# Loading batch 0 in four pieces, the taps ahead of conv1's weights, and one step of the taps' transform in front of the first transposes

## The chip, the cores and the metric

The kernel runs on one core of a Trainium2 chip. The metric is the device time of one execution in microseconds (us). The kernel before takes 1845.73 us, median of its first three runs (1843.53 to 1846.13). All runs told of here are of the state fast. With them comes, to three digits, the mean clock granted to TensorE during the run.

## The reference, cut to what matters

One layer of a graph network on 32 graphs of 512 nodes and 256 features, in float32.

```python
h = jnp.maximum(_layernorm(x, axis=-1), 0.0)
# inside the layer, with x now being h:
xc = jnp.transpose(x, (0, 2, 1))
h = relu(_bn(_conv1d(xc, conv1_w, 0), ...))      # a 256 x 256 product per node
h = _bn(_conv1d(h, conv2_w, 8), ...)             # 17 taps along the nodes
x_conv = transpose(relu(h + xc))
# ... message passing over adj, then a GRU cell; the result is added to x
```

## The kernel before

The 17-tap convolution is done by Fourier transforms of windows. Two things have to be transformed: the activations, batch by batch (`px`), and the taps of conv2, once (`pw`). The taps' transform comes in 32 steps of four matmuls each (eight records in the trace), which the kernel spreads over the loop that prepares the first 16 batches. The loop's TensorE work per batch is conv1 (`pc`), a step of the taps, the window transform of the batch before (`px`), a second step, and the transposes of the next batch (`phT`).

One step, and who takes its results out of PSUM (`s` is 0 for an even step and 2 for an odd one):

```python
def weights_to_freq(gen, pc, i):
    s = i % SI                                   # SI = 4 channels to a group of four buffers
    if s == 0:
        for q in range(4):                       # a new group: 8 buffers, so two groups
            WST[q] = gen.tile([ROWS, SI, D], FP, tag="wst", ..., bufs=8)
    for q in range(4):
        p = bank(...)                            # one of 8 PSUM banks
        nc.tensor.matmul(p[:ROWS, :], taps[...], W2P[pc][...], start=True, stop=True)
    for q in range(4):
        if (pc or i >= SI) and (q == 3 or (q == 1 and s == 0)):
            nc.vector.tensor_copy(dst, src)      # even step: two, odd step: one
        else:
            nc.scalar.copy(dst, src)             # even step: two, odd step: three
    if s + per == SI:                            # after the odd step: store the group
        for q in range(4):
            nc.sync.dma_start(WD[...], WST[q]...)
```

The loads at the start, and which steps a batch gets:

```python
nc.scalar.dma_start(vec, vecs)
nc.scalar.dma_start(fwd, ...)                    # window transform
nc.scalar.dma_start(taps, ...)                   # taps' transform
# ... (cut)
load_w1()                                        # conv1's weights, four transfers on ScalarE's queue
load_x(0)                                        # 512 KB each, on SyncE's queue
load_x(1)
load_taps(gen, 0, nc.sync)                       # first 8 of 64 channels per quarter, five transfers

def between(b):
    # ... every second batch: load the next taps; batches 1 to 7: load a late weight
    mine = spread(steps, b, GB - 1) if b < GB - 1 else []
    return mine[:1], mine[1:]                    # one after conv1, the rest after px
```

Of the kernel before, what the change touches and what calls it, by code (L numbers as in the profile page):

```python
# [11 lines left out]
FP = mybir.dt.float32  # L12
# [3 lines left out]
P = 128  # L16
# [49 lines left out]
def gnn_layer(  # L66
# [15 lines left out]
    nc = tc.nc  # L82
    B, N, D = x.shape
# [45 lines left out]
    nc.scalar.dma_start(vec, vecs)  # L129
    w1 = early.tile([P, DC, D], FP, name="w1")  # L130
    fwd = early.tile([P, 2 * L], FP, name="fwd")
    nc.scalar.dma_start(fwd, nc.inline_tensor(fwd_np, name="dft_fwd").ap())
    taps = early.tile([P, ROWS], FP, name="taps")
    nc.scalar.dma_start(taps, nc.inline_tensor(taps_np, name="dft_taps").ap())
    back = consts.tile([P, back_np.shape[1]], FP, name="back")
# [53 lines left out]
    def load_w1():  # L189

        t = W2P["w1"] = pools["gen"].tile([P, PI, D], FP, tag="w2p", name="w1_in", bufs=2)
        load_rows(t[:, :DC], w1T, nc.scalar)

    def scale_w1():
        t = W2P.pop("w1")
# [615 lines left out]
    def first_part(g, freq, between, left=()):  # L811


        b0, b1 = g * GB, (g + 1) * GB
        for b in range(b0, b0 + 3):
            if b not in X and (g == 0 or b == b0):
                load_x(b)
        if g == 0:
            t = XN[b0] = pools["first"].tile([P, NC, D], FP, tag="xn", name="rows", bufs=2)
            ones, diags = t[:, 0, :P], t[:, 1:3, :].rearrange("p i (c m) -> p i c m", m=P)  # L820
            nc.vector.memset(ones, 1.0)

            for _ in range(6):
                nc.tensor.matmul(row1[1][:, : 2 * P], ident, fr.rearrange("p c g k -> p (c g k)")[:, : 2 * P], start=True, stop=True)
            batch_norm("bn1", scale1, shift1, nc.gpsimd)
            bn1_row(0, scale1, ones, diags)
            bn1_row(1, shift1, ones, diags)
        if b0 not in STATS:
            statistics(b0)
        normalise(b0)  # L830
        if g == 0:
            scale_w1()
            shift_w1()
        left = list(left)

        def fill():
            for step in left.pop(0) if left else ():
                step()

        if g > 0:  # L840
            load_x(b0 + 1)
            fill()
            load_x(b0 + 2)
        transpose_h(b0)
        fill()
        statistics(b0 + 1)
        if g > 0:
            statistics(b0 + 2)
        normalise(b0 + 1, g > 0)
        fill()  # L850
        for b in range(b0, b1):
            if b + 3 < b1:
                load_x(b + 3, nc.gpsimd)
            if b == b0:
                conv1(b)
                one, two = between(0) if g == 0 else ([], [])
                for step in one:
                    step()
                fill()
                if g == 0:  # L860
                    transpose_h(b + 1)
                    statistics(b + 2)
                    normalise(b + 2)
                else:
                    normalise(b + 2)
                    transpose_h(b + 1)
                fill()
                xf, last_two = freq(g), two
                continue
            if g == 0 and b == b0 + 1:  # L870
                conv1(b)
                for step in last_two:
                    step()
            if b + 2 < b1:
                statistics(b + 2)
            if b + 1 < b1:
                transpose_h(b + 1)
            if b + 2 < b1:
                normalise(b + 2)
            one, two = between(b - b0)  # L880
            if b > b0 + (g == 0):
                conv1(b)
            if b == b1 - 1:
                load_h(b0)
            for step in one:
                step()
            windows_to_freq(b - 1, xf)
            for step in two:
                step()
        by_chunks(b1 - 1)  # L890
        load_h(b0 + 1)
        windows_to_freq(b1 - 1, xf)
        by_chunks(b0)
        return xf
# [8 lines left out]
    with tc.tile_pool(name="freq", bufs=1) as fpool:  # L903
        def freq_tile(g):
            return fpool.tile([P, DC, L, P], FP, tag="xf", name=f"xf_{g}")

        with phase("first", "gen"):
            gen = pools["gen"]
            per = N // D
            steps = [partial(weights_to_freq, gen, pc, i) for pc in range(QI // PI) for i in range(0, PI, per)]  # L910
            load_w1()
            load_x(0)
            load_x(1)
            load_taps(gen, 0, nc.sync)

            def between(b):
                if b % 2 == 0 and b // 2 + 1 < QI // PI:
                    load_taps(gen, b // 2 + 1)
                if 1 <= b <= len(load_weights):
                    load_weights[b - 1]()  # L920
                mine = spread(steps, b, GB - 1) if b < GB - 1 else []
                return mine[:1], mine[1:]

            with tc.manual_schedule():
                xf = first_part(0, freq_tile, between)

                for u in range(3):
                    load_unit(0, u)


        LEFT = 4

        def nodes(g, xf, units, last):


            b1 = (g + 1) * GB
            todo = [b1 - 1] + list(range(g * GB, b1 - 1))
            def begin(i):
                if i < GB:
                    if todo[i] not in HQ:  # L940
                        by_chunks(todo[i])
                    message(todo[i])
                    features(todo[i])

            load_adj(todo[0])
            with tc.manual_schedule():
                begin(0)
                message(todo[1])
                factors(todo[0])
                features(todo[1])  # L950
            affinity(todo[0])
            for i, b in enumerate(todo):
                mine = spread(units, i, last) if i < last else []
                more = i + 1 < GB

                if g + 1 < NG and i == GB // 2:
                    load_x(b1)
                if g + 1 < NG and i == 3 * GB // 4:
                    statistics(b1)
                if i + 2 < GB and todo[i + 2] not in HT:  # L960
                    load_h(todo[i + 2])
                if more:
                    load_adj(todo[i + 1])
                    factors(todo[i + 1])

                parts = [range(DC)] if mine or not more else [[0], [1]]
                if len(parts) > 1:
                    aggregate(b, parts.pop(0))
                for u in mine[:1]:
                    product(pools["pw"], g, u, xf)  # L970
                begin(i + 2)
                if more:
                    affinity(todo[i + 1])
                for u in mine[1:2]:
                    product(pools["pw"], g, u, xf)
                aggregate(b, *parts)
                save_nmp(b)
                for u in mine[2:]:
                    product(pools["pw"], g, u, xf)

        with phase("pw", "ahead"):
            with phase("nodes"):
                nodes(0, xf, range(UNITS - LEFT), GB)
            with phase("first", "sums"):
                combine = combine_weights()

                def between(b):

                    if b == GB - 3:
                        for u in range(3):  # L990
                            load_unit(1, u)
                    two = [partial(sum_unit, pools["pw"], 1, b - GB + 3)] if b > GB - 3 else []
                    return combine[b - 1] if 0 < b <= len(combine) else [], two


                pw, (u0, u1, u2, u3) = pools["pw"], range(UNITS - LEFT, UNITS)
                left = [[partial(load_unit, 0, u2, pools["sums"])],
                        [partial(prepare, pw, 0, u1, xf), partial(product, pw, 0, u0, xf), partial(prepare, pw, 0, u2, xf)],
                        [partial(product, pw, 0, u1, xf), partial(load_unit, 0, u3)],
                        [partial(prepare, pw, 0, u3, xf), partial(product, pw, 0, u2, xf)],  # L1000
                        [partial(product, pw, 0, u3, xf)]]
                prepare(pw, 0, u0, xf)
                load_unit(0, u1)
                with tc.manual_schedule():
                    xf = first_part(1, freq_tile, between, left)
            with phase("nodes"):
                nodes(1, xf, range(UNITS), GB - 3)
# [76 lines left out]
```

## Time and profile before

| | before |
|---|---|
| median time | 1845.73 us |
| TensorE busy | 99% of the span |
| TensorE in the chain that ended last | 89% |
| batches 2 to 6, each | 9.27 us |
| batch 7 (three steps) | 10.38 us |
| batches 8 to 13, each | 9.66 us |

The time of a batch is the distance between the starts of conv1 of two batches in TensorE's row of the timeline. The lines behind this table are in the prediction below.

### The profile page before, as it was taken

To read this page: it belongs to the slowest core of one execution; us is meant where nothing else is said; L and a number is where in the kernel's file an instruction comes from. 1 tells how busy PE (TensorE), PEld (TensorE's weight loads), DVE (VectorE), ACT (ScalarE), POOL (GpSimd) and SP (SyncE) were. 2 spreads that over 40 slices of the span, in tenths; PEclk is the share of its full clock that TensorE was granted. 3 is DMA by queue.
4 is the path that set the end of the run, shared out by engine and by line. 5 is a ranking of instruction groups with operands and counts; after the bars stand their busy time and mean duration, and the time that the engine had idled before them with its cause. 6 is when DMAs were issued, how large, how long until landed. Compare 5 with 4: busy or idle time off the path is not lost.

```text
span 1848.1 us, 20105 instructions
## 1 busy us (share of the span) xinstructions
PE 1826.4 (99%) x6610; PEld 1089.0 (59%) x6610; DVE 1109.1 (60%) x2220; ACT 581.9 (31%) x1083; POOL 588.2 (32%) x572
## 2 busy tenths in 40 slices
PE   9999999999999999999999999999999999999998
PEld 6777666666888666665555554555455544555443
DVE  7775656554885555545266466655666466645666
ACT  4555434432335333333222221222122221222121
POOL 3331333333432344444422323133212322133221
PEclk9999999999999999999999999999999999999999
DMA  8999888875678887778421443234422442244312
GB/s 233 299 276 241 225 226 246 218 179 180 212 250 207 235 245 235 216 207 261 123 86 34 120 120 99 53 88 120 120 78 43 120 120 88 49 103 120 112 25 52
DMA packets 307452, 289.26 MB, mean 157 GB/s; under 512 B 148028, under 2 KB 237148, under 8 KB 306964
## 3 DMA queue, kind: packets, MB, share of 16 engines
q1 hardware_dynamic: 281300, 224.22, 46.0%
q10 hardware_dynamic: 19024, 38.68, 5.9%
q0 software_dynamic: 7024, 25.07, 4.8%
q8 instruction: 53, 0.87, 0.2%
q14 instruction: 51, 0.42, 0.1%
HBM read 191.50 MB, written 96.40 MB: 156 GB/s over the span
## 4 chain that ended last, share of the span: by engine, by line
PE 89%; DVE 4%; issue 3%; DMA 2%; POOL 1%; ACT 1%; SPq 0%; POOLq 0%; ACTq 0%; DVEq 0%
PE pg L597 29%; PE pn L597 14%; PE pn L489 11%; PE py L393 11%; PE pm L439 6%; PE pc L585 5%; PE pc L328 3%; PE px L343 3%; PE pw L256 2%; PE pd L474 2%; PE phT L312 1%; DMA w<-in_w_ihT_dram 1%; PE psr L463 1%; DVE stats L285 1%; DVE xn L304 1%
## 5 line engine op out<-in xcount | busy, mean ns | idle before, releaser
L489 PE MATMUL pn<-A,msg 128*128 128x512 f32 x512 | 225.9, 593 | 0.6 <-DVE A L480 0.6
L597 PE MATMUL pg<-hp,sw 128*128 128x512 f32 x434 | 221.8, 593 | 0.7 <-DVE rz L616 0.5
L597 PE MATMUL pg<-np,sw 128*128 128x512 f32 x434 | 221.6, 592 | 0.0
L597 PE MATMUL pg<-cp,sw 128*128 128x512 f32 x434 | 221.6, 592 | 0.0
L575 POOL TENSOR_TENSOR hp<-hp 128x512 f32<-128x512 f32 x64 | 81.3, 1280 | 413.0 <-DMA hp<-hd 234.6
L372 POOL TENSOR_TENSOR both<-xf 128x256 f32<-128x256 f32 x78 | 60.1, 771 | 329.1 <-PE py L393 297.5
L489 PEld LDWEIGHTS pn<-A,msg 128*128 128x128 f32 x512 | 97.2, 191 | 110.9 <-issue 105.7
L575 POOL TENSOR_TENSOR cp<-cp 128x512 f32<-128x512 f32 x64 | 80.4, 1267 | 229.8 <-ACT cp L591 228.6
L393 PE MATMUL py<-wt,both 128*128 128x256 f32 x624 | 151.0, 385 | 0.7 <-issue 0.7
L612 ACT ACTIVATE rz<-rz,brz 128x512 f32<-128x512 f32 x93 | 67.0, 721 | 260.2 <-DVE rz L616 260.2
L400 DVE TENSOR_TENSOR y<-y,py 128x256 f32<-128x256 f32 x78 | 31.8, 408 | 190.5 <-ACT y L399 185.8
L597 PEld LDWEIGHTS pg<-hp,sw 128*128 128x128 f32 x434 | 82.2, 190 | 104.8 <-issue 97.8
L597 PEld LDWEIGHTS pg<-cp,sw 128*128 128x128 f32 x434 | 82.5, 190 | 103.8 <-issue 103.8
L597 PEld LDWEIGHTS pg<-np,sw 128*128 128x128 f32 x434 | 82.5, 190 | 103.8 <-issue 103.8
L393 PEld LDWEIGHTS py<-wt,both 128*128 128x128 f32 x624 | 114.3, 190 | 43.2 <-issue 28.3
L480 DVE TENSOR_TENSOR A<-e,at 128x512 f32<-128x512 f32 x128 | 114.5, 933 | 36.9 <-ACT e L477 36.7
L359 POOL TENSOR_TENSOR wsum<-wt 128x512 f32<-128x512 f32 x78 | 109.1, 1399 | 51.8 <-DMA wt<-wd 39.1
L735 ACT ACTIVATE nt<-nt,vech 128x512 f32<-128x512 f32 x64 | 46.2, 722 | 235.8 <-DVE nt L734 235.8
L328 PE MATMUL pc<-w,hT 128*128 128x256 f32 x512 | 116.7, 381 | 1.6 <-DVE hT L316 1.6
L439 PE MATMUL pm<-wmsg,hq 128*128 128x259 f32 x512 | 117.5, 382 | 0.6 <-ACT sl L460 0.6
L597 PE MATMUL pn<-np,sw 128*128 128x512 f32 x224 | 114.4, 592 | 0.0
L597 PE MATMUL pn<-cp,sw 128*128 128x512 f32 x224 | 114.4, 592 | 0.0
(146 smaller groups left out, 2963.6 us busy)
## 6 DMA issues: line engine op xcount, KB each, us to landing
wt<-wd SPq DMA_DIRECT2D x160, 256.0 KB, 4.3
adj<-in_adj_dram SPq DMA_DIRECT2D x128, 256.0 KB, 5.4
wd<-wst SPq DMA_DIRECT2D x64, 320.0 KB, 5.3
yd<-y ACTq DMA_DIRECT2D x80, 256.0 KB, 4.3
yt<-yd SPq DMA_DIRECT2D x30, 640.0 KB, 7.5
hd<-hT SPq DMA_DIRECT2D x32, 512.0 KB, 4.4
nd<-nmp ACTq DMA_DIRECT2D x32, 512.0 KB, 4.0
xb<-in_x_dram SPq DMA_DIRECT2D x128, 128.0 KB, 3.8
```

Of the source, the lines that this page charges most:

```text
L328: nc.tensor.matmul(p[:, j, :], HT[b][:, ic, c * P : (c + 1) * P], w1[:, ic, :], start=(ic == 0), stop=(ic == DC - 1))
L343: nc.tensor.matmul(p[:, j * 2 * L : (j + 1) * 2 * L], H1[b][:, c0 + j, ic * P : (ic + 1) * P], fwd, start=True, stop=True)
L359: nc.gpsimd.tensor_tensor(t, WT[g, u][:, 0], WT[g, u][:, 1], op=ALU.add)
L372: nc.gpsimd.tensor_tensor(both[:, 0], re, im, op=ALU.add)
L393: nc.tensor.matmul(dst, v[:, ic, :], w[:, ic, :], start=(ic == 0), stop=(ic == DC - 1))
L439: nc.tensor.matmul(p[:, : D + NS], hq[:, ic, c * P : (c + 1) * P], wmsg[:, ic, :], start=(ic == 0), stop=(ic == DC - 1))
L480: nc.vector.tensor_mul(A[b][:, mc, :], e, at)
L489: nc.tensor.matmul(p, MSG[b][:, mc, dc * P : (dc + 1) * P], A[b][:, mc, :], start=(mc == 0), stop=(mc == NC - 1))
L575: nc.gpsimd.tensor_tensor(t[:, dst, :], t[:, a, :], t[:, b, :], op=sub)
L585: nc.tensor.matmul(bk[:, t0:t1], YT[p][j][:, c, oc * P : (oc + 1) * P], back[:, n : n + t1 - t0], start=(c == 0), stop=(c == len(spans) - ...
L597: nc.tensor.matmul(bk[:, t], sw[:, k, q, o, :], terms[k][q][:, t], start=(first and i == 0), stop=(i == len(ks) - 1), skip_group_check=True)
L612: nc.scalar.activation(rz[:, g, j, :], src, AF.Sigmoid, bias=brz[:, g : g + 1], scale=1.0)
```

## The change

The intent: TensorE stands idle several times in the first 11 us. Batch 0 should come sooner by being split over two queues, its statistics should start with the first piece, and an idle place in front of the first transposes should be filled with a step of the taps that the loop then need not do.

```diff
-    nc.scalar.dma_start(fwd, ...)               # now last on ScalarE's queue
     nc.scalar.dma_start(taps, ...)
 # ... in load_w1
-        load_rows(t[:, :DC], w1T, nc.scalar)
+        load_rows(t[:, :DC], w1T, nc.sync)
 # ... in first_part, group 0
             batch_norm("bn1", scale1, shift1, nc.gpsimd)
+            statistics(b0)
             bn1_row(0, scale1, ones, diags)
             bn1_row(1, shift1, ones, diags)
+            left.pop(0)[0]()                    # step 0 of the taps
 # ... the loads
+            X[0] = pools["first"].tile([P, NC, D], FP, tag="x", name="x_0", bufs=3)
+            for c in range(NC):
+                (nc.sync if c % 2 == 0 else nc.scalar).dma_start(X[0][:, c, :], x[0, c * P : (c + 1) * P, :])
+            load_taps(gen, 0, nc.sync)
             load_w1()
-            load_x(0)
             load_x(1)
-            load_taps(gen, 0, nc.sync)
+            nc.scalar.dma_start(fwd, ...)
 # ... (cut)
-                xf = first_part(0, freq_tile, between)
+                xf = first_part(0, freq_tile, between, [[steps.pop(0)]])
```

A side effect is not visible in the diff: `between` now spreads 31 steps instead of 32. Every batch from 0 to 6 gets the pair (odd, even) where it had (even, odd).

More of the change, by code (lines that the diff above doesn't have):

```diff
@@ L131, in gnn_layer @@
     fwd = early.tile([P, 2 * L], FP, name="fwd")
-    nc.scalar.dma_start(fwd, nc.inline_tensor(fwd_np, name="dft_fwd").ap())
     taps = early.tile([P, ROWS], FP, name="taps")
@@ L817, in first_part @@
                 load_x(b)
+        left = list(left)
         if g == 0:
@@ L833, in first_part @@
             shift_w1()
-        left = list(left)
         def fill():
@@ L910, in gnn_layer @@
             steps = [partial(weights_to_freq, gen, pc, i) for pc in range(QI // PI) for i in range(0, PI, per)]
+            X[0] = pools["first"].tile([P, NC, D], FP, tag="x", name="x_0", bufs=3)
+            for c in range(NC):
+                (nc.sync if c % 2 == 0 else nc.scalar).dma_start(X[0][:, c, :], x[0, c * P : (c + 1) * P, :])
+            load_taps(gen, 0, nc.sync)
             load_w1()
-            load_x(0)
             load_x(1)
-            load_taps(gen, 0, nc.sync)
+            nc.scalar.dma_start(fwd, nc.inline_tensor(fwd_np, name="dft_fwd").ap())
             def between(b):
```

## The prediction

> **What bounds the kernel now.** I read the page's busy shares first, then the chain of work that ended last, then the same chain for the first 40 us alone, because the whole diff acts before and inside the loop over the first 16 batches.
>
> ```profile
> PE 1826.4 (99%) x6610; PEld 1089.0 (59%) x6610; DVE 1109.1 (60%) x2220; ACT 581.9 (31%) x1083; POOL 588.2 (32%) x572
> ...
> PE 89%; DVE 4%; issue 3%; DMA 2%; POOL 1%; ACT 1%; SPq 0%; POOLq 0%; ACTq 0%; DVEq 0%
> ```
>
> TensorE is 89% of the chain. Outside its idle places, the only way to win is to take away TensorE work or a stall of it. The change takes away none: the taps' transform still has 32 steps of eight matmul records. It moves one. So I look for idle places in the first microseconds (chain of waits, window 0 to 40 us; columns: start, length, what):
>
> ```profile
> 0.72 4.20 DMA x<-in_x_dram
> ...
> 5.30 1.28 ACT L186
> ...
> 8.44 1.31 PE phT L312 x4
> ...
> 9.84 0.75 DVE w L197 x2
> 10.59 0.60 DVE hT L316
> 11.19 1.31 DVE stats L285 x4
> ...
> 23.26 1.23 ACT h L332 x2
> ...
> 25.00 2.19 PE pw L256 x3
> 27.19 4.57 PE px L343 x16
> ```
>
> The reader should see four things. Batch 0 (512 KB) is waited for until 4.93 us. The scaling of conv1's weights on VectorE starts at 9.84, and the trace has the last piece of those weights landing at 9.76, so that landing, not the matmul named as releaser, holds it. From 10.59 to 24 us the chain is VectorE, GpSimd and ScalarE, not TensorE. And the 16 `px` matmuls take 4.57 us there against 2.37 in every later batch. The table by stage says why (columns: window, length, busy time of PE, PEld, DVE, ACT, POOL, granted clock, DMA share, GB/s):
>
> ```profile
> 26.00:34.00 8.00, 8.00 (x35) 5.43 (x33) 4.09 (x9) 3.81 (x9) 1.56 (x2) 0.58 0.91 281
> 34.26:80.63 46.37, 46.37 (x282) 33.63 (x281) 37.34 (x102) 24.58 (x57) 17.67 (x25) 1.00 0.99 297
> 80.63:91.01 10.38, 10.38 (x66) 7.50 (x65) 8.42 (x23) 6.21 (x15) 3.98 (x10) 1.00 0.84 255
> 91.01:148.95 57.94, 57.94 (x338) 41.12 (x337) 45.08 (x121) 29.70 (x67) 17.93 (x25) 1.00 0.93 272
> ```
>
> The clock was 0.58 from 26 to 34 us. The other three rows are batches 2 to 6, batch 7 and batches 8 to 13, cut where conv1 of a batch starts. Five batches take 46.37 us, 9.27 each; batch 7 takes 10.38; six batches take 57.94, 9.66 each. Each has two steps of the taps, batch 7 three. So a batch of two steps is not always equally long, and the cause sits in the second step (timeline, batch 5 and then batch 9):
>
> ```profile
> 68.02 1.05 ACT L266 COPY wst<-pw 80x512 f32<-80x512 f32 x2
> 68.84 1.69 PE L256 MATMUL pw<-w2p,taps 17*80 17x512 f32 x8
> ```
>
> ```profile
> 106.74 1.53 ACT L266 COPY wst<-pw 80x512 f32<-80x512 f32 x3
> 107.52 1.88 PE L256 MATMUL pw<-w2p,taps 17*80 17x512 f32 x8
> ```
>
> Even steps put two of their four copies out of PSUM on VectorE, odd steps one. Through batch 6 each batch runs (even, odd): the first step leaves ScalarE two copies, 1.05 us. After the triple of batch 7 each batch runs (odd, even): three copies, 1.53 us. The second step's banks are those of the first (four `pw`, four `px`, eight banks), so it waits longer for ScalarE: 1.75 to 1.91 us in place of 1.27 (even batches) to 1.69 (odd ones).
>
> **What the Trainium skill says.** "DMA: Bandwidth & Descriptors", section "Issuing engines are not separate DMA queues": transfers started by different engines run on the same 16 DMA engines, and using several issuers saves only issue time. The trace agrees as far as it goes: each issue of `x` takes 0.45 to 0.51 us of its queue, and the DMA share is full from about 2.6 us. The same page, section "Anatomy of one DMA", gives a fixed part of about 2.0 us for the GpSimd path; here, on ScalarE's queue, the 14 KB of `vec` took 2.6 us from issue to landing. "Perfetto Trace Analysis", section "DMA Optimizations", says that splitting may let some pieces start sooner if the DMA engines are generally idle; they are idle here only for the first 2 us. "TensorE: Matmul & The Clock Gate", Part 1, says that the array's clock is halved after an idle window of about 3.4 us: the half-clock stretch in the trace lasts 6.8 us, two such windows, and follows a place where the second `pw` step of batch 1 takes 3.72 us for 1.03 us of work.
>
> **The change part by part.**
>
> *Batch 0 in four pieces.* Pieces 0 and 2 are issued on SyncE at about 0.72 and 1.2 us, pieces 1 and 3 on ScalarE behind `vec` and the transform constants, at about 1.7 and 2.15. With the 2.6 us of `vec` as a floor they should land near 3.5, 3.9, 4.4 and 4.9 (estimate from those issue times). The last is no earlier than 4.93, but statistics no longer wait for the whole: four at 0.33 us end near 5.3 in place of 6.3. VectorE's normalisation then starts near 7.0 instead of 7.97: 1.0 us won on that branch. ScalarE, rid of four conv1 weight issues (3.12 us, to 5.27), can load its table before 4.8, and its diagonals start at about 5.2 instead of 6.59. Both gains count only if nothing later takes over.
>
> *Taps ahead of conv1 weights.* The taps come as 4 x 128 + 32 = 544 KB. In the trace their issues on SyncE wait for earlier landings (waits of the SyncE queue):
>
> ```profile
> SPq L243 <- DMA taps<-dft_taps: 2.0, 1, 2.0
> SPq L243 <- DMA vec<-in_vecs_dram: 1.6, 1, 1.6
> SPq L243 <- DMA fwd<-dft_fwd: 1.5, 1, 1.5
> ```
>
> There seem to be eight completion slots: each issue waits for the one eight before. The slots are now held by small early transfers, so I expect taps issues at about 1.7 to 5 us. The DMA moved 202, 158 and 131 GB/s in 6 to 8, 8 to 10 and 10 to 12 us, when taps and conv1 weights dominated. At 150 GB/s the taps need 3.6 us, so they are all there at about 8.2. The conv1 weights (256 KB) follow, 1.7 us more: 9.8 to 10 us, where they are today (9.76). Batch 1 then needs 1.5 us at about 340 GB/s: 11.3 to 11.5, against its statistics at 11.11 today.
>
> *One step in front of the transposes.* Eight matmuls, 1.03 us, from 8.2 to 9.3. Transposes follow densely (1.03 us) to 10.35; today they end at 10.18. Four copies of 0.5 us go onto ScalarE ahead of the shift row (0.37) and its half of the first `hT` (0.60): 8.6 + 2.0 + 0.37 + 0.60 = 11.6 against 10.81. So conv1 of batch 0 starts about 0.4 later in its second operand. **Start: +0.4 us.**
>
> *The remaining 31 steps, two per batch.* Batches 0 and 1 run steps 1 to 4 in place of 0 to 3. By the code (steps 0 and 1 put all four copies on ScalarE) ScalarE gets 11 of these 16 copies instead of 13, and VectorE, itself in the chain, 5 instead of 3. I put the relief of the 3.72 us step at 1.3 us, half of its 2.7 us stall, because VectorE pays some back. **Batches 0 and 1: -1.3 us.** Batches 2 to 6 take the (odd, even) order: 5 x (9.66 - 9.27) = **+1.9 us.** Batch 7 has two steps instead of three: 9.66 - 10.38 = **-0.7 us.** Batches 8 on keep the order they have.
>
> *Clock.* If the shorter stall leaves the window busy enough, the half-clock stretch disappears: it costs about 2.2 us in `px` (4.57 against 2.37) and some 0.5 in the step after it, 3 us with the rest of the window. I give that three chances in ten: **-0.9 us.**
>
> Sum: 0.4 - 1.3 + 1.9 - 0.7 - 0.9 = -0.6. From 1845.73 that is **1845.1 us**.
>
> **The rivals.** First, the plain intent: a free step of 1.0 us in an idle place, batch 0 sooner, and nothing paid: -1 to -2.5 us, 1843.5 us. For it: TensorE has about 0.6 + 0.7 + 1.1 us idle before conv1. Against it: the order of the steps flips in the loop, and the later batches of this very trace show what that costs. Second, conv1's weights become the bound: behind the taps at only 100 GB/s they would land near 11.5, conv1 and VectorE's chain would start 1.5 us later, and the result is 1847 to 1848. For it: the weights already hold VectorE today; taps and weights move at half the rate of `x`. Against it: batch 1's 512 KB no longer lie ahead of them. Third, the clock alone: if the stretch goes, 1842 to 1843; if a second one comes because TensorE sits idle waiting for the taps, 1848 to 1849. Fourth, a late tap piece in the loop: the odd batches now need the next eight taps one step sooner. The second load lands at 48.2 us in the trace, and the step would be due at about 50, so it is close but should hold.
>
> **Range and chances.** The terms are each uncertain by about a microsecond and the clock by three, in opposite directions, and the three runs of before spread over 2.6 us. Eight times in ten I expect 1842.3 to 1848.5. Two per cent is 37 us; nothing here is that large. Faster by over 2%: 0.01; within 2%: 0.98; slower: 0.01.
>
> **What would show it.** Right: conv1's weights land at 9.5 to 10.5 us and VectorE's scaling starts right then; ScalarE's four `wst` copies lie ahead of the first `hT`; batches 2 to 6 take 9.6 to 9.7 us each, with three ScalarE copies before the second step; batch 7 takes the same. Wrong: batches 2 to 6 still at 9.27 (then the order is not the cause); TensorE waiting over 2 us for the taps; a granted clock of 1.00 through 26 to 34 us, or a new low stretch elsewhere, which would outweigh all my other terms; or a difference that arises after 160 us, which nothing here accounts for.

## The result, and the profile after

The changed kernel takes 1852.53 us (median of 4 runs, 1851.22 to 1854.55) beside 1844.93 us of before (4 runs). The ratio is 1.0042, with a 95% interval from 1.0025 to 1.0060. Ratios here are the mean time of one kernel's fast runs over that of the other's of the same rounds, so not quite the ratio of the medians. By the 2% rule this is the same; but it lies clear of the noise and outside the predicted range, on the slow side.

The page of the changed kernel hardly differs (busy shares, first line of each view):

```profile
PE 1826.5 (99%) x6610; PEld 1087.9 (59%) x6610; DVE 1107.6 (60%) x2220; ACT 581.7 (31%) x1083; POOL 588.5 (32%) x572
...
PE 88%; DVE 4%; DMA 3%; issue 2%; POOL 1%; ACT 1%; SPq 0%; POOLq 0%; ACTq 0%; DVEq 0%
```

TensorE did the same 6610 matmul records in the same time. DMA has risen from 2% to 3% of the chain. The chain of the first 60 us shows where:

```profile
5.08 4.98 DMA w2p<-in_w2T_dram
...
10.83 1.11 PE pw L255 x8
11.94 2.01 ACT wst L265 x4
13.95 0.27 ACT shift_row L200
14.22 0.50 ACT hT L313
...
14.77 5.68 PE pc L327 x14
...
31.35 2.37 PE px L342 x16
...
36.70 9.01 DMA wd<-wst
...
48.27 8.57 DMA wd<-wst
```

And TensorE's and VectorE's rows at the start (start, length, engine, line, what; in brackets how long the engine was idle before it, and for what):

```profile
10.83 1.10 PE L255 MATMUL pw<-w2p,taps 17*80 17x512 f32 x8 [3.20 <-DMA w2p<-in_w2T_dram]
11.68 0.75 DVE L196 TENSOR_TENSOR w<-w_in,row 128x256 f32<-128x256 f32 x2 [0.93 <-DMA w_in<-in_w1T_dram]
```

Three things are to be seen. The start now hangs on the taps: the fourth of their five transfers lands at 10.06 us, the fifth at 10.74, and step 0 begins at 10.83, not at 8.2. Conv1's weights land at 11.55, and VectorE's scaling starts right behind them. After step 0 come the four copies and the shift row on ScalarE, and conv1's second operand waits for them until 14.77, as the prediction had it but 3 us later. And two stores of transformed weights, 9.0 and 8.6 us long, are in the chain, which before held none.

The stages (columns as in the prediction: window, length, busy times, granted clock, DMA share, GB/s). The last three rows are batches 2 to 6, batch 7 and batches 8 to 13, from one conv1 start to another:

```profile
12.80:19.60 6.80, 6.20 (x15) 4.37 (x14) 4.54 (x15) 2.55 (x6) 4.47 (x7) 0.50 0.51 175
26.00:34.00 8.00, 7.95 (x48) 4.47 (x50) 7.56 (x21) 5.13 (x11) 2.92 (x4) 1.00 0.68 218
35.61:86.63 51.02, 49.83 (x283) 34.55 (x281) 38.47 (x103) 24.59 (x56) 17.66 (x25) 1.00 1.00 283
86.63:96.28 9.65, 9.65 (x59) 6.87 (x58) 7.62 (x21) 4.92 (x12) 4.23 (x10) 1.00 0.90 281
96.28:154.22 57.94, 57.94 (x338) 41.05 (x337) 44.84 (x121) 29.54 (x67) 17.95 (x25) 1.00 0.91 269
```

The half-clock stretch has not gone; it has moved from 26 us to 12.8 us, onto conv1 of batch 0. Batch 7 takes 9.65 us and batches 8 to 13 take 57.94, both as predicted. Batches 2 to 6 take 51.02 us instead of 46.37, where 48.3 was predicted, and TensorE is busy in only 49.83 of them. ScalarE does leave three copies ahead of the second step there, as predicted (batch 4; the second step starts at 64.41):

```profile
63.80 1.53 ACT L265 COPY wst<-pw 80x512 f32<-80x512 f32 x3
```

VectorE's waits from 30 to 165 us name what is new; the kernel before has no such line:

```profile
DVE wst L263 <- DMA wd<-wst: 3.7, 3, 1.9
```

The starts of conv1, read from TensorE's row of the timeline, of these two kernels and of the runs below (us):

| run | batch 0 | batch 1 | batch 2 | batch 8 | batch 14 | 2 to 8 | 8 to 14 |
|---|---|---|---|---|---|---|---|
| before | 11.24 | 17.60 | 34.10 | 90.85 | 148.79 | 56.75 | 57.94 |
| before_again | 11.29 | 17.66 | 32.53 | 89.29 | 147.22 | 56.76 | 57.93 |
| changed | 13.40 | 22.85 | 35.61 | 96.28 | 154.22 | 60.67 | 57.94 |
| after_again | 12.81 | 22.19 | 34.95 | 95.62 | 153.55 | 60.67 | 57.93 |
| loads_only | 12.86 | 21.92 | 35.21 | 91.93 | 149.87 | 56.72 | 57.94 |
| pairs_kept | 12.07 | 19.14 | 34.01 | 92.28 | 150.23 | 58.27 | 57.95 |
| pairs_shifted | 11.40 | 17.76 | 32.45 | 96.13 | 154.07 | 63.68 | 57.94 |
| weights_later | 12.81 | 22.13 | 34.89 | 93.85 | 151.67 | 58.96 | 57.82 |
| split_swapped | 14.24 | 21.79 | 36.70 | 93.04 | 147.63 | 56.34 | 54.59 |
| warm | 14.07 | 21.17 | 33.92 | 94.86 | 152.81 | 60.94 | 57.95 |
| pieces_only | 14.53 | 22.51 | 37.42 | 94.17 | 152.11 | 56.75 | 57.94 |
| pieces_sync | 12.87 | 20.68 | 35.59 | 92.34 | 150.30 | 56.75 | 57.96 |
| after_sync | 14.10 | 21.50 | 35.93 | 97.58 | 155.52 | 61.65 | 57.94 |
| even_pairs | 11.10 | 17.46 | 32.34 | 88.12 | 143.69 | 55.78 | 55.57 |
| even_two_two | 11.16 | 17.52 | 32.43 | 89.67 | 146.56 | 57.24 | 56.89 |
| shifted_swapped | 11.21 | 17.56 | 35.53 | 96.40 | 151.01 | 60.87 | 54.61 |
| even_pairs_again | 11.12 | 18.93 | 33.78 | 89.58 | 145.15 | 55.80 | 55.57 |
| even_pieces_sync | 13.62 | 21.27 | 36.18 | 91.97 | 147.53 | 55.79 | 55.56 |
| swapped_later | 12.64 | 19.00 | 37.19 | 92.13 | 146.85 | 54.94 | 54.72 |

By batch 14 the changed kernel is 6.3 us behind before_again in its second trace (153.55 against 147.22): 2.4 us by batch 2 and 3.9 us from batch 2 to 8. After that nothing in the traces belongs to the change: from conv1 of batch 14 to the end the two traces of before take 1699.3 and 1699.5 us, those of the changed kernel 1695.2 and 1699.8. Over all 19 traces this rest lies between 1693.8 and 1707.9 us, and it tends to be longer where the trace has more half-clock time between 160 and 1800 us (3.4 to 13.7 us; correlation 0.77). The whole times carry this scatter too.

### The profile page after: what moved, and what is told of

It is laid out like the page before. It is cut to its first block, busy times and chain, and to the rows that moved or that the text cites. A ratio compares the mean times of both kernels' runs of the same rounds, so it can differ in the third digit from the quotient of the medians.

```text
span 1849.4 us, 20106 instructions
## 1 busy us (share of the span) xinstructions
PE 1826.5 (99%) x6610; PEld 1087.9 (59%) x6610; DVE 1107.6 (60%) x2220; ACT 581.7 (31%) x1083; POOL 588.5 (32%) x572
## 3 DMA queue, kind: packets, MB, share of 16 engines
HBM read 191.50 MB, written 96.40 MB: 156 GB/s over the span
## 4 chain that ended last, share of the span: by engine, by line
PE 88%; DVE 4%; DMA 3%; issue 2%; POOL 1%; ACT 1%; SPq 0%; POOLq 0%; ACTq 0%; DVEq 0%
PE pg L596 29%; PE pn L596 14%; PE pn L488 12%; PE py L392 11%; PE pm L438 6%; PE pc L584 5%; PE pc L327 3%; PE px L342 2%; PE pd L473 2%; PE pw L255 2%; DMA w<-in_w_ihT_dram 1%; DMA wd<-wst 1%; PE phT L311 1%; DVE stats L284 1%; PE psr L462 1%
## 5 line engine op out<-in xcount | busy, mean ns | idle before, releaser
L358 POOL TENSOR_TENSOR wsum<-wt 128x512 f32<-128x512 f32 x78 | 108.4, 1391 | 48.3 <-DMA wt<-wd 38.2
```

Of the source, the lines that this page charges most:

```text
L358: nc.gpsimd.tensor_tensor(t, WT[g, u][:, 0], WT[g, u][:, 1], op=ALU.add)
```

## The experiments

My theory after the result: the loss is a late start (the loads) plus the turned order of the steps, which costs more than I had put down because VectorE waits for stores. The rivals: the new loads disturb the DMA queues in the loop and the order is innocent; or the start is everything and carries through; or the clock is everything.

Each kernel below ran six times, its profiled run among them. The profile shows one execution; the times show all six, and they differ by up to 13 us within one kernel. So small verdicts rest on the table above, and the times are the check on it.

### before_again: what chance does

The unchanged kernel.

> The kernel before, unchanged, for a second trace and for the noise. The first trace of it comes from an execution of 1849.9 us, which is 5 us above the median of its other runs, and it has three half-clock stretches (25.8, 176.0 and 223.8 us) where the changed kernel has two (12.8 and 224.4). If the clock stretches of the first trace were a matter of chance, this trace has fewer of them and conv1 of batch 2 starts at about 31.5 us instead of 34.1. If they belong to the kernel, it has the same three. Time 1845 us within 1.5 either way.

Measured: 1847.63 us (1845.39 to 1851.16) beside 1845.90 of the runs of before; ratio 1.0012 (0.9993 to 1.0030). Its trace has a half-clock stretch at 26.4 us again, but only half as long (3.4 us), none at 176, and conv1 of batch 2 starts at 32.53 instead of 34.10. So the stretch at 26 us belongs to the kernel, its length and the later stretches vary. From batch 2 on the batches agree to 0.02 us.

All executions of the kernel before in experiments, these six and the 55 that ran beside the others, 61 in number, lie between 1840.2 and 1852.6 us and follow their mean granted clock:

| mean clock | runs of before | mean us |
|---|---|---|
| 0.994 | 2 | 1850.1 |
| 0.995 | 18 | 1848.8 |
| 0.996 | 18 | 1847.1 |
| 0.997 | 17 | 1845.2 |
| 0.998 | 6 | 1842.4 |

A straight line through the 61 runs gives 2.0 us per 0.001 of clock. That is my ruler for "at equal clock" below. It is an estimate and no more: the clock is given to three digits, and half clock while TensorE is idle lowers it without cost. It doesn't carry over to every kernel: by it, `warm` below would stand 7 us above before at equal clock, more than the changed kernel, though its trace is less far behind by batch 14 (5.6 us against 6.3, both beside before_again).

### loads_only and pairs_kept: undoing the step, undoing the turned order

```diff
 # loads_only, against the changed kernel: no step in front, 32 steps spread as before
-            left.pop(0)[0]()
-                xf = first_part(0, freq_tile, between, [[steps.pop(0)]])
+                xf = first_part(0, freq_tile, between)
 # pairs_kept, against the changed kernel: step 0 in front, then 1 | 2,3 | 4,5 | ...
+                if b == 0:
+                    return mine[1:], []
-                xf = first_part(0, freq_tile, between, [[steps.pop(0)]])
+                xf = first_part(0, freq_tile, between, [[steps[0]]])
```

> The changed kernel's loads and the earlier statistics, but every step of the taps in its old place and old pairs. My theory (the loss is a late start plus the turned order of the steps in the loop): only conv1's weights, landing near 11.5 us instead of 9.8, hold the start, so 1.5 to 2.5 us over before: 1846.5 to 1847.5, and batches 2 to 6 at 9.2 to 9.3 us. Rival A (the new loads disturb the DMA queue in the loop, the order of steps is innocent): VectorE still waits for the stores of the transformed weights in batches 2 to 4, 1849 us or more.

> The changed kernel with step 0 in front, but batch 0 then runs step 1 alone and every later batch runs the pair it ran before (2 and 3, 4 and 5, three steps in batch 7). My theory: the waits for stores in batches 2 to 4 go, those batches fall to about 9.3 us, and about 4 us of the 7.6 come back: 1848 to 1849. Rival A: no change, 1852. Rival B (nearly all of the loss is the start, which then carries through): no change either, but the batches would show 9.3 us with the same total.

loads_only took 1849.22 us (1843.93 to 1850.77) beside 1845.90, ratio 1.0014 (0.9994 to 1.0033); pairs_kept 1851.45 (1847.73 to 1856.32), ratio 1.0026 (1.0006 to 1.0046). With the old order the loop is the old one: 56.72 us from batch 2 to 8 in loads_only, no wait for a store. In pairs_kept it is 58.27, but 1.5 us of that are in batch 2 alone, where a half-clock stretch (30.7 to 37.5 us) happened to fall; its batches 3 to 7 are 9.57, 9.08, 9.50, 9.09 and 10.38 us against 9.49, 9.09, 9.50, 9.09 and 10.39 in before_again. That refutes the rival of disturbed queues in the loop. The loads alone already start conv1 of batch 0 1.6 us late and conv1 of batch 1 4.3 us late; half clock falls on it at 12 us, and the stretch at 26 us is then missing, so 2.7 us of lag are left at batch 2. My times were too low for both, and pairs_kept's median is only 1.1 us under the changed kernel's, though its trace is 3.3 us ahead of after_again by batch 14: its rest after that is 1704.3 us, with half clock for 13.7 us of it.

### pairs_shifted: the turned order alone

```diff
 # against the kernel before: batch 0 runs 0 | 1,2, then 3,4 | 5,6 | ...
-                mine = spread(steps, b, GB - 1) if b < GB - 1 else []
+                mine = spread(steps[1:], b, GB - 1) if b < GB - 1 else []
+                if b == 0:
+                    mine = steps[:1] + mine
```

> The kernel before, with nothing changed but the order: batch 0 runs steps 0, 1 and 2, so that each later batch runs an odd step and then an even one, as in the changed kernel. My theory: the loop alone loses 3 to 4 us, batches 2 to 4 at 10 us or more with VectorE waiting for stores: 1848 to 1849. Rivals A and B: within a microsecond of before, 1845 to 1846.

Measured: 1856.24 us (1853.72 to 1858.00) beside 1845.90; ratio 1.0056 (1.0038 to 1.0074). This was the largest effect, larger than I expected, and it comes from the order of the same matmuls alone. From batch 2 to 8 it takes 63.68 us instead of 56.76; batch 4 takes 13.37. The chain and VectorE's row show the store in it (VectorE's row: start, length, engine, line, what; in brackets how long the engine was idle and for what):

```profile
43.88 9.88 DMA wd<-wst
```

```profile
53.85 0.69 DVE L264 COPY wst<-pw 80x512 f32<-80x512 f32 x1 [2.15 <-DMA wd<-wst]
54.46 1.39 DVE L285 BATCH_NORM_STATS2 stats<-x 128x6 f32<-128x256 f32 x4
```

The copy into a `wst` buffer stands in VectorE's queue in front of the statistics. While it waits for the store that frees the buffer, everything behind it waits too. Half clock fell on the late batches after that (from 62 us), which is part of the 13.37.

The order matters to the stores because of the distance between closing a group and opening the one after next. In the old order a group is opened by the first step of a batch and stored after the second. Its buffers are wanted again by the first step of the batch two later. In the turned order it is opened by the second step of one batch and stored after the first step of the next; it is wanted again by the second step of the batch after that. An estimate from the rows of batch 5 of the kernel before, 9.5 us long: copies of the first step run from 67.4 to 69.1 us, those of the second from 70.2 to 71.8. So the old order leaves 67.4 + 2 x 9.5 - 71.8 = 14.6 us for the store, the turned one 70.2 + 2 x 9.5 - (69.1 + 9.5) = 10.6. In the changed kernel the stores between 30 and 70 us took 7.9 us in the middle and up to 10.0 from issue to landing, and the four of a group are issued one after the other.

### weights_later and split_swapped: the stores, and ScalarE's third copy

```diff
 # weights_later, against the changed kernel
-                if 1 <= b <= len(load_weights):
-                    load_weights[b - 1]()
+                if 8 <= b < 8 + len(load_weights):
+                    load_weights[b - 8]()
 # split_swapped, against the changed kernel: odd steps give VectorE two copies, even ones one
-            if (pc or i >= SI) and (q == 3 or (q == 1 and s == 0)):
+            if (pc or i >= SI) and (q == 3 or (q == 1 and s != 0)):
```

> The changed kernel with the loads of the late weights (416 KB of the back transform, the message weights, vectors) moved from batches 1 to 7 to batches 8 to 14. Theory: in the turned order a group of transformed weights is opened in one batch and closed in the next, so its store has about 4 us less until its buffers are wanted again; the store is slow in batches 2 to 4 because those loads share the queue. Then VectorE's waits for the stores go there and batches 2 to 4 fall from 10.6, 10.0 and 11.1 us to about 9.7: 2 to 3 us less than the changed kernel, about 1850. Rival: the stores wait for something else (the taps, the batches' own rows); then batches 2 to 4 stay above 10 us.

> The changed kernel with the two-copy share of VectorE given to the odd steps instead of the even ones, so that in the turned order the first step of each batch again leaves ScalarE two copies. Theory: what is left of the loss in batches 6 to 13 (9.65 us against 9.1 to 9.5) is ScalarE's third copy; those batches fall to 9.1 to 9.5, about 0.35 us each, while the store waits of batches 2 to 4 stay at least in part. 3 to 4 us less than the changed kernel, 1849. Rival: the length of these batches has another cause (the taps' loads, the banks); they stay at 9.65.

weights_later took 1852.49 us (1849.65 to 1854.00) beside 1846.93, ratio 1.0026 (1.0013 to 1.0040). All waits of VectorE of any size from 30 to 165 us in it:

```profile
DVE wst L263 <- PE pw L255: 25.7, 13, 2.6
DVE h L330 <- PE pc L327: 3.8, 4, 1.0
DVE wst L263 <- ACT xf L345: 2.0, 1, 2.0
```

The wait for stores is gone, and batches 3 and 4 fall from 10.01 and 11.08 us to 9.73 and 9.58. The stores between 30 and 70 us took 7.0 us in the middle instead of 7.9. So the late weights' loads made the stores slow enough to be waited for, and the store waits were 1.7 us of the 3.9, by one trace. Batch 2 stays at 10.63: there three copies stand ahead of VectorE's statistics in the chain, a pile-up of VectorE and not a store. (It goes with the split of the copies: in split_swapped batch 2 takes 9.20.) The expected total of 1850 was missed in the median.

split_swapped took 1847.09 us (1843.23 to 1849.49) beside 1846.93, ratio 0.9997 (0.9982 to 1.0011): with one comparison turned, the loss of the changed kernel is gone from the time. The start stays late (conv1 of batch 2 at 36.70); it is made up for in the loop. From batch 2 to 8 it takes 56.34 us, 4.3 less than the changed kernel and about what before takes, and it then gains 3.3 us in batches 8 to 13, where before runs (odd, even) pairs with a third copy too (window row):

```profile
93.04:147.63 54.59, 54.59 (x338) 39.74 (x337) 44.62 (x121) 29.54 (x67) 17.92 (x25) 1.00 0.95 288
```

54.59 us instead of 57.94, or 9.10 a batch instead of 9.66, more than I expected. ScalarE's third copy between the two steps is thereby shown to be what the turned order costs where no store waits. The 4.3 us here and the 1.7 of weights_later are not to be added up: two store waits remained, 4.7 us in all, and batch 4 took 10.42.

### warm: the half-clock stretch at the start

```diff
-            for _ in range(6):
+            for _ in range(14):
```

> The changed kernel with 14 instead of 6 of the matmuls that TensorE does at the start for nothing, so that it is busy to about 10 us and not idle from 7.6 to 10.8. Theory: the half-clock stretch from 12.8 to 19.6 us comes from that idle time; it goes, conv1 of batch 0 takes 3.7 us instead of 5.9, and conv1 of batch 1 starts at about 20.5 instead of 22.9. At the end of the first 16 batches 1 to 2 us less than the changed kernel, if no other stretch comes. Rival: the stretch has nothing to do with it and stays.

Measured: 1853.47 us (1850.70 to 1859.06) beside 1846.93; ratio 1.0035 (1.0017 to 1.0052). The mechanism came as expected: the stretch at 12.8 us is gone (the window 12.8 to 19.6 has a granted clock of 1.00), and the rest of conv1 of batch 0 takes 3.29 us where it took 5.68:

```profile
15.48 3.29 PE L327 MATMUL pc<-w,hT 128*128 128x256 f32 x14 [0.73 <-ACT hT L313]
```

By batch 2 it is 1.7 us ahead of the changed kernel. The time shows nothing of it: the runs are as slow as the changed kernel's, at a higher mean clock (0.996 against 0.995). Filling the idle time in front of step 0 with matmuls for nothing does not make the kernel faster here. That this idle time brings on the half clock fits most of the traces and not all: of seven with these loads, five show it from 10 to 13 us on, and pairs_kept, idle for only 1.47 us before step 0, and warm do not; yet split_swapped has it after 2.24 us, and even_pairs_again, with the loads of before, has 3.4 us of it from 11.7 us on. So chance has a part in it.

### after_again: how much of the 7.6 us is the clock's luck

> The changed kernel, unchanged, on the chip of the other runs of this call. The 28 runs of before so far lie between 1840 and 1851 us and follow their mean granted clock: 1849.1 at 0.995, 1847.0 at 0.996, 1845.0 at 0.997. If the loss is in the kernel, the changed one is slower at the same clock too: 5 us or more above before in the median, 1851 to 1853, and batches 2 to 5 again over 10 us in part. If the first 7.6 us were partly the clock's luck, the difference of the medians shrinks to 4 to 6.

Measured: 1855.90 us (1848.29 to 1857.42) beside 1847.14; ratio 1.0045 (1.0027 to 1.0063). So the loss is no accident; my guess that it might shrink was wrong. The ten runs of the changed kernel have a mean of 1854.0 us at a mean clock of 0.9947; the 61 of before 1846.7 at 0.9961. With the ruler, 0.0014 of clock is 2.8 us, and 4.5 us remain at equal clock. Whether the lower clock is itself made by the idle places that the change brings, or partly chance, these runs do not settle.

### pieces_only, pieces_sync and after_sync: what makes the start late

```diff
 # pieces_only, against the kernel before: the pieces on both queues, everything else in its place
-            load_w1()
-            load_x(0)
+            X[0] = pools["first"].tile([P, NC, D], FP, tag="x", name="x_0", bufs=3)
+            for c in range(NC):
+                (nc.sync if c % 2 == 0 else nc.scalar).dma_start(X[0][:, c, :], x[0, c * P : (c + 1) * P, :])
+            load_w1()
 # pieces_sync: pieces_only, and after_sync: the changed kernel, each with
-                (nc.sync if c % 2 == 0 else nc.scalar).dma_start(X[0]...)
+                nc.sync.dma_start(X[0]...)
```

> The kernel before with batch 0 in four pieces on the two queues and nothing else: conv1's weights still on ScalarE's queue, batch 1 and then the taps on SyncE's, steps in their old places. If the pieces themselves cost the start (in the changed kernel the last piece landed at 7.3 us instead of 4.9), the statistics end at about 7 us and conv1 starts later than 11.3. If it is the taps ahead of conv1's weights, the weights land near 9.8 as before and conv1 starts at 11.0 to 11.5. Time within 1 us of before in either case but for the clock.

> The kernel before with batch 0 in four pieces, all on SyncE's queue ahead of batch 1. If sharing the DMA engines with the other queue held the pieces back, the last one lands at 5 us or sooner, the statistics end 0.5 to 1 us sooner than before, and conv1 of batch 0 starts at 11.0 to 11.5, held by conv1's weights. Time within 1.5 us of before. Rival: pieces as such are slow; then the last lands at 7 us or later again.

> The changed kernel with its four pieces all on SyncE's queue. The pieces are all there by 5 us, but the taps still land at about 10 and step 0 still stands in front of the transposes: conv1 of batch 0 starts at 12.5 to 13.5 and the half-clock stretch near 12 us stays. So no gain: 1852 to 1856. If the pieces were the whole of the late start, conv1 would start at about 11.5 and 2 us come back.

pieces_only took 1852.11 us (1849.08 to 1854.85) beside 1847.14, ratio 1.0033 (1.0016 to 1.0049). This I had not expected: the split alone, the part of the change that looks safest, costs 5.0 us in the median, and its trace is 4.9 us behind before_again by batch 2. VectorE's row, first of the changed kernel and then of pieces_only:

```profile
2.92 0.43 DVE L284 BATCH_NORM_STATS2 stats<-x 128x6 f32<-128x256 f32 x1 [1.17 <-DMA x<-in_x_dram]
6.24 0.75 DVE L284 BATCH_NORM_STATS2 stats<-x 128x6 f32<-128x256 f32 x2 [2.89 <-DMA x<-in_x_dram]
7.32 0.43 DVE L284 BATCH_NORM_STATS2 stats<-x 128x6 f32<-128x256 f32 x1 [0.33 <-DMA x<-in_x_dram]
```

```profile
3.10 0.43 DVE L285 BATCH_NORM_STATS2 stats<-x 128x6 f32<-128x256 f32 x1 [1.34 <-DMA x<-in_x_dram]
8.40 0.75 DVE L285 BATCH_NORM_STATS2 stats<-x 128x6 f32<-128x256 f32 x2 [4.88 <-DMA x<-in_x_dram]
9.79 0.43 DVE L285 BATCH_NORM_STATS2 stats<-x 128x6 f32<-128x256 f32 x1 [0.63 <-DMA x<-in_x_dram]
```

The first piece is there at 2.9 us in both, and the pieces of ScalarE's queue come at 6.2 and 7.3, or at 8.4 and 9.8. They are issued between 1.7 and 2.7 us, when SyncE's queue already holds something large: the taps in the changed kernel, batch 1 in pieces_only (issued at 1.67 us, landed at 9.44). As one transfer, with batch 1 behind it in the same queue, all of batch 0 was there at 4.93 (4.9 to 5.5 us in the eight traces with that load).

pieces_sync puts all pieces on SyncE's queue, and the last one lands at 5.55 us. That is 4.2 us sooner than on two queues, though later than the 5 us that I had expected; in even_pieces_sync it was 6.70. The time is that of before: 1847.66 us (1843.78 to 1851.60) beside 1847.54, ratio 1.0002 (0.9979 to 1.0025). Conv1 still starts at 12.87, not at 11.0 to 11.5, because the last piece of conv1's weights now lands at 11.23: the taps are issued from 3.8 to 5.7 us instead of from 3.7 to 7.9 (before_again) and run beside it. Why the earlier landing of batch 0 was paid for with just this transfer I did not test.

after_sync took 1854.06 us (1848.89 to 1858.44) beside 1847.54, ratio 1.0040 (1.0016 to 1.0063): no gain over the changed kernel, as expected. The last piece landed at 6.26 there, not by 5, but step 0 waits for the taps until 10.17 all the same. In the changed kernel one queue does not even bring the last piece sooner: in the seven traces with its loads it landed at 6.0 to 7.3 us. There the taps hold step 0, conv1's weights land about as late, and the pieces are hidden behind both. It is beside batch 1, as in pieces_only, that two queues were bad.

### even_pairs, even_two_two, shifted_swapped and swapped_later: is there something better

```diff
 # even_pairs, against the kernel before: (0,1) (2,3) ... to the end, four steps in batch 14
-                mine = spread(steps, b, GB - 1) if b < GB - 1 else []
+                mine = steps[2 * b : 2 * b + 2] if b < GB - 2 else steps[2 * b :] if b < GB - 1 else []
 # even_two_two: even_pairs and
-            if (pc or i >= SI) and (q == 3 or (q == 1 and s == 0)):
+            if (pc or i >= SI) and q in (1, 3):
 # shifted_swapped: pairs_shifted with the split of split_swapped
 # swapped_later: shifted_swapped with the loads of weights_later
```

> The kernel before with the pairs (0,1), (2,3), ... kept through all batches: batch 7 gets two steps, batch 14 four. If the order (even, odd) is what makes a batch 9.3 us and (odd, even) 9.65, batches 8 to 13 fall to 9.1 to 9.5 and the first 16 batches end about 2 us sooner than in the kernel before: 1843. If not, they stay at 9.65 and the time at 1845.

> Even pairs in all batches once more. From the batches (9.27 us each instead of 9.66 for six of them, 2.1 us in all) 2 us less than before at the same clock, ratio 0.9985 to 0.9995; if the first result was the clock's luck, the ratio is 1.000 or above.

> Even pairs in all batches, and batch 0 in four pieces on SyncE's queue. Like even_pairs, with at most 0.5 us more from the start: 1844 to 1845 beside a before of 1846.5.

even_pairs took 1844.68 us (1842.67 to 1848.07) beside 1846.93, ratio 0.9987 (0.9973 to 1.0000), and at the second try 1846.84 (1842.17 to 1850.26) beside 1847.54, ratio 1.0000 (0.9978 to 1.0022). Batches 8 to 13 fall as expected, to 9.26 us each:

```profile
88.12:143.69 55.57, 55.57 (x338) 40.36 (x337) 44.62 (x121) 29.53 (x67) 17.91 (x25) 1.00 0.92 275
```

Its batch 14 with four steps takes 10.69 instead of 8.84, so about 1.5 us are won on the loop. That is within the noise of six runs. even_pieces_sync, which adds pieces on one queue, took 1848.46 us beside 1847.54, ratio 1.0007 (0.9984 to 1.0029): nothing gained.

> The kernel before with even pairs in all batches, and every step from the third on with two copies on VectorE and two on ScalarE. ScalarE then has two copies after the first step and after the second. If ScalarE is all that lengthens a batch, batches 2 to 13 fall from 9.27 to about 9.05, 2.5 us in all, on top of the 2 us of even pairs: 1842 to 1843. Rival: VectorE, which has one more copy per batch, becomes the bound; then the batches stay at 9.3 or rise.

even_two_two took 1851.04 us (1846.17 to 1856.26) beside 1847.14, ratio 1.0025 (1.0007 to 1.0043). As the rival had it, there is no gain: odd batches rise to 9.8 to 9.9 us with VectorE busy for 8.67 of 9.94, and even ones are at 9.08. Whether VectorE is the bound there is not shown, for the chain of batch 9 also holds a store of 4.73 us. Of the splits tried with the even step first, two copies on VectorE in the even steps alone was the better one.

> The kernel before with the turned order (batch 0 runs steps 0, 1 and 2) and the two-copy share given to the odd steps. If the turned order costs time only through ScalarE's third copy and the stores, batches 6 to 13 take 9.1 us and only batches 2 to 5 keep store waits: 1845 to 1848, against 1856 of the turned order alone. Rival: the turned order has a further cost; 1850 or more.

> The kernel before with the turned order, the two-copy share on the odd steps, and the late weights loaded in batches 8 to 14. If store waits and the third copy are all that the turned order costs, batches 3 to 13 take 9.0 to 9.2 us with no wait for a store, conv1 of batch 14 starts at 142 to 144 us instead of 147.2, and at equal clock the time is 3 us under before: 1843 to 1845. Rival: the store waits come back elsewhere (the taps' loads); then batches 4 or 5 stay over 10 us and the time is 1847 or more.

shifted_swapped took 1849.61 us (1844.51 to 1857.69) beside 1847.14, ratio 1.0019 (0.9998 to 1.0040), with 9.1 us in batches 7 to 13 and long batches 4 and 5 (13.72 and 10.43 us), with half clock from 64 to 71 us among them. swapped_later has no store wait, and its twelve batches from 2 to 13 are the best of all:

```profile
37.19:146.85 109.66, 109.66 (x674) 79.70 (x673) 89.57 (x242) 59.17 (x133) 39.30 (x60) 1.00 0.97 287
```

109.66 us against 114.69 in before_again. So store waits and the third copy are together the whole cost of the turned order in the loop: without them it is 5.0 us faster than the old one. But the time was 1848.31 us (1843.23 to 1851.85) beside 1846.67, ratio 1.0006 (0.9990 to 1.0021). The distance from conv1 of batch 1 to that of batch 2 was 18.2 us in place of 14.9, with half clock from 28 to 35 us, and conv1 of batch 0 began 1.3 us late in this trace. No version is shown to beat the kernel before; the changed kernel is beaten by it and, in the median, by most of these.

## Why the prediction was wrong

The prediction was 1845.1 us with a range to 1848.5. The changed kernel took 1852.53 and, in a second set, 1855.90.

**The step that failed** is the first term of the sum, "Start: +0.4 us", together with "5 x (9.66 - 9.27) = +1.9 us" for batches 2 to 6. The first had the wrong size because the landing times under it were wrong: conv1 of batch 0 starts 1.5 to 2.2 us late, and conv1 of batch 2 is 2.4 us late, where start and batches 0 and 1 together were to gain 0.9. The second had the right sign and the cost of the third copy, but left out the waits for stores: it measured +4.65 us.

- *Pieces at 3.5, 3.9, 4.4 and 4.9 us.* Those of ScalarE's queue were needed and there at 6.2 and 7.3 (5.4 and 6.1 in after_again). I had taken the time of a small transfer on an empty machine for a floor and then used it as the value. I had even quoted that all issuers share the same DMA engines, and did not ask what would lie in the other queue at that moment. (Nor were those engines full from 2.6 us: in the finer view of before they are half busy from 1.6 us and full from about 3.2. And of the three issues of `x` one took 0.40 us, not all of them 0.45 or more.)
- *All taps at 8.2 us.* Step 0 started at 10.83. I had put their 3.6 us at 150 GB/s and from about 4.6 us on, as if batch 0 were done by then and nothing ran beside them. From 6 to 10 us the DMA engines moved 131 GB/s, and the last pieces, the window transform's constants and conv1's weights had their share of that. The fourth taps issue waited until 5.08 for the completion of an earlier transfer, as the prediction had described in general.
- *Conv1's weights at 9.8 to 10 us.* They landed at 11.55, behind the taps. This was the second rival's mechanism with the second rival's time. In the changed kernel step 0 nearly hides it, but it is enough by itself: loads_only has no step there and starts conv1 at 12.86, against 12.81 in after_again.
- *Four copies ahead of the first `hT` on ScalarE.* Right: conv1's second operand comes behind exactly this, at 14.72 instead of 11.6. TensorE was idle for it for only 0.18 us at half clock, and for 0.73 us in warm at full clock.
- *Batches 0 and 1: -1.3 us.* Between batches 1 and 2 the changed kernel needs 12.76 us against 14.87 in before_again and 16.50 in the first trace of before. Most of that is half clock which lies elsewhere. loads_only, with the old steps and no half clock there, needs 13.29, and its second `pw` step of batch 1 takes 3.10 us where the changed kernel's takes 2.63. So the relief is there, but 0.5 us and not 1.3.
- *Batches 2 to 6: +1.9 us.* They cost 4.65 us more (51.02 against 46.37). ScalarE's third copy was right, as split_swapped shows. Missing were the stores: two groups of `wst` buffers, reopened sooner in the turned order (pairs_shifted, weights_later), and the pile-up of VectorE in batch 2. I had checked the taps for lateness in the turned order, and not the store at the other end of the same step.
- *Batch 7: -0.7 us.* Right: 9.65 us. Batches 8 to 13 unchanged at 57.94: right.
- *Clock: -0.9 us.* Wrong. The stretch moved to 12.8 us, into conv1, as the third rival and the last paragraph had allowed. The idle time ahead of step 0 favours it (warm), though not in every trace (pairs_kept).

Of the prediction's own signs of being wrong, two came: TensorE waited 3.20 us for the taps, and a low stretch arose elsewhere. No difference arose after 160 us, and the fourth rival did not come either: from 30 to 165 us TensorE has no wait for the taps.

The sum by batch 8, after_again against before_again: +2.4 for the start and +3.9 for the loop, 6.3 us, where the same terms of the prediction without the clock give 0.4 - 1.3 + 1.9 - 0.7 = +0.3. The first three runs of before were also somewhat lucky: 61 later ones have a median of 1847.0.

What stays open: why the changed kernel's mean clock is lower over the whole run (0.9947 against 0.9961), although its traces do not have more half-clock stretches every time; and which of its parts would have to go to get that back.

## What to carry to other kernels

Moving one item to the front of a list that is dealt out in pairs turns every pair after it: look at what the order inside a pair decides (which engine empties the banks, when a buffer is opened and stored) before counting the matmuls saved. A transfer split over two queues is not ahead of what the other queue holds (pieces_only); put urgent pieces ahead in the one queue where bulk follows them (pieces_sync), and count all the bytes that must arrive by a given time. For effects of a few microseconds compare stages in two traces of the same kernel first, and whole times only beside their granted clock.

## What the Trainium skill lacked or had wrong

- "DMA: Bandwidth & Descriptors", section "Issuing engines are not separate DMA queues", says that a second issuer saves only issue time. It does not say that it can cost: with pieces 1 and 3 on ScalarE's queue, beside 512 KB on SyncE's, they landed at 8.4 and 9.8 us (one trace), where the whole 512 KB of the batch had landed at 4.9 to 5.5 us and four pieces on one queue at 5.6 to 6.7.
- "Perfetto Trace Analysis", section "DMA Optimizations", ties splitting to idle DMA engines. The runs agree (they were busy here, and four pieces on one queue gained nothing: ratio 1.0002), but its next point, balancing over issuing engines where an issuer is the bottleneck, gives no warning of the loss above.
- "TensorE: Matmul & The Clock Gate", Part 1, calls the ramp penalty under 1% of a typical span. That holds (mean granted clock 0.994 to 0.998). But no section says how far whole times spread by it: runs of one unchanged kernel spread from 1840.2 to 1852.6 us (0.7%), and 0.001 of mean clock goes with 2.0 us.
